# Eight buffers of e, denominators eight slots behind a chunk's end, weight bands in every sixth slot

## The chip, the cores and the metric

The kernel runs on one core of one Trainium2 chip. The time is the device time of one execution in microseconds, the median of several executions. One further execution was recorded by the hardware profiler; the views quoted below are of that one.

## What is computed

Two layers run on x of shape (2, 256, 64, 64) in fp32. Layer 0 is global attention over all 4096 pixels with eight heads of 32 channels, a fusion of the result with x by a 1x1 convolution, and a blend by a mask. Layer 1 is a channel gate, attention inside windows of 8x8 pixels, a shuffle of channels and two grouped 7x7 convolutions that make a gate.

```python
# layer 0, per image
q, k, v = proj(Wq, bq) / sqrt(32), proj(Wk, bk), proj(Wv, bv)
fuse = softmax(q @ k.T) @ v                      # 8 heads, 4096 x 4096
hybrid = conv1x1(concat([x, fuse]), Wf, bf)
x = hybrid * m + x * (1 - m)
# layer 1
x = x * sigmoid(relu(x @ ca_w1 + ca_b1) @ ca_w2 + ca_b2)
x = x + window_attention(x) @ out_w + out_b      # 8x8 windows, 4 heads
x = shuffle_channels(x)
y = relu(bn(grouped_conv7x7(x, sa_w1)))
y = bn(grouped_conv7x7(y, sa_w2))
out = x * sigmoid(y)
```

## The kernel before

A first phase projects q, k and v and stores them in DRAM. Then comes one long loop over 1024 *slots* (the for loop at L1015). A slot is one (image b, chunk c of 512 queries, group g of four heads, block m of 128 keys). With 2 images, 8 chunks, 2 groups and 32 blocks, a *chunk* is 64 slots, and there are 16 chunks. After the loop follows a tail with the last chunk's stage and the convolutions.

In slot i the loop issues the following, and the order in which instructions are issued here is the order in which each engine runs them; nothing is rearranged later.

- `scores(i + 2)`: four matmuls of k against q into PSUM (L578), and three exponentials on ScalarE into a buffer e of 128x2048 values (L588). The pool of e has `EB` = 5 buffers (L31, L585).
- `products(i)`: four matmuls of e against v that accumulate over the 32 blocks in one PSUM bank (L607), and one VectorE addition of e onto a running sum (L609), which makes the softmax denominators. The first slot of a group has no addition, since the second adds the first two e. A buffer of e is free for slot i + 5 when the matmuls and the addition of slot i are done.
- In the last slot of group 1 (slot 63 of a chunk) further work is queued with `at(delay, ...)`, which sets how many slots later it is issued: `denominators` (L630, 32 small matmuls that sum over keys, and a copy), the reciprocal on VectorE (L658), two `spread` steps (L645, matmuls that spread the reciprocals over the heads' channels, and a copy), and the product of f with the reciprocals on VectorE (L661).
- Seven slots after a chunk's end the chunk's `stage` (L664) is put in a list, and in every fourth slot the loop advances it by one of its fourteen steps (up to the next `yield`). The first step is the fusion (L674), whose matmuls read x first and then f; it ends by issuing the load of the next x on SP's queue (L518), which waits until VectorE has read the old x (L688). Later steps are the channel gate, the window attention with 16 small exponentials (L799), and last the two VectorE additions into `xo` (L861) with its stores to `x_s` (L876), nearly all on POOL's queue. The list's first step runs in slot 72 counted from the chunk's start, its last in slot 124, that is slot 60 of the next chunk.
- Loads of k and v pieces (four blocks each) go through SP's queue (L505, L507), two pieces ahead, with three buffers.
- `bands()` (L415) writes the two convolutions' weights into banded matrices `w_s` in DRAM: 156 DMAs on POOL's queue (L424, L430, L437), one in every second slot. They depend on nothing that the loop computes. The convolutions in the tail read `w_s` (L905).

POOL's queue is in order, so the band writes stand there between the stores of `xo`, which wait for VectorE.

Of the kernel before, what the change touches and what calls it, by code (L numbers as in the profile page):

```python
# [27 lines left out]
PB = 4  # L28
NPIECE = NMB // PB
AHEAD = 2  # L30
EB = 5  # L31
WB = 8
HEADS1, HD1 = 4, 64
WS = 8
# [20 lines left out]
def conv_seq_kernel(ctx: ExitStack, tc: tile.TileContext, a, out):  # L55
    nc = tc.nc
# [13 lines left out]
    def psum2(name):  # L70
        return ps["pair"].tile([P, 2, CH], F32, tag="s", name=name)
# [114 lines left out]
    with (  # L186
# [19 lines left out]
        for b in range(B):  # L206
            src = a["x"][b].rearrange("(k p) h w -> p k (h w)", p=P)
            for c in range(NCHUNK):
# [55 lines left out]
                i = b * NCHUNK + c  # L264
# [145 lines left out]
    def spread(row, n):  # L410
        f = row.shape[-1]
        return row.rearrange("p u f -> u p f").to_broadcast([NU, n, f])
# [58 lines left out]
    def pipeline(arm, shifted, pools):  # L471
# [4 lines left out]
        qp = att.enter_context(tc.tile_pool(name=f"q{arm}", bufs=2))  # L476
        ep = att.enter_context(tc.tile_pool(name=f"e{arm}", bufs=EB))

# [14 lines left out]
        stages = deque()  # L493

        def at(delay, action):
            later.append((now[0] + delay, action))

        def load_piece(n):
            if n * PB >= len(slots):
                return  # L500
            b, c, g, m = slots[n * PB]
            p = m // PB
            nm_ = f"{arm}_{b}_{c}_{g}_{p}"
            k = kvp.tile([P, PB * P], F32, tag="k", name=f"k{nm_}")
            nc.sync.dma_start(k, k_s[b, g, p])  # L505
            v = kvp.tile([P, PB, P], F32, tag="v", name=f"v{nm_}")
            nc.sync.dma_start(v, v_s[b, g, p].rearrange("p (m d) -> p m d", m=PB))  # L507
            kts[b, c, g, p], vts[b, c, g, p] = k, v

        def load_q(b, c):  # L510
            q = qp.tile([P, KC, CH], F32, tag="q", name=f"q{arm}_{b}_{c}")
            nc.sync.dma_start(q, q_s[b, c].rearrange("p (g n) -> p g n", g=KC))
            qts[b, c] = q
# [52 lines left out]
        def scores(i):  # L566
            b, c, g, m = slots[i]
            if shifted and m == 0:
                shift[0] = row_max(b, c, g)
            k, q = kts[b, c, g, m // PB], qts[b, c]  # L570
            cols = slice((m % PB) * P, (m % PB + 1) * P)
            one, pair = psum1(f"s{arm}_{i}_0"), psum2(f"s{arm}_{i}_1")
            last = psum1(f"s{arm}_{i}_2")
            heads = [one, pair[:, 0, :], pair[:, 1, :], last]
            parts = [(one, 0), (pair, slice(1, 3)), (last, 3)]
            for j in range(HG):
                r = slice(32 * j, 32 * j + 32)
                nc.tensor.matmul(heads[j], k[r, cols], q[r, g, :], start=True, stop=not shifted)  # L578
            if shifted:
                for j in range(HG):  # L580
                    r = slice(32 * j, 32 * j + 1)
                    nc.tensor.matmul(
                        heads[j], ones[r, :], shift[0][r, :], start=False, stop=True
                    )
            e = es[i] = ep.tile([P, HG, CH], F32, tag="e", name=f"e{arm}_{i}")  # L585

            def exp(tile, h):
                nc.scalar.activation(e[:, h, :], tile, AF.Exp, scale=SCALE0)  # L588

            for part in parts[:-1]:  # L590
                exp(*part)

            return lambda: exp(*parts[-1])


        def products(i):
            b, c, g, m = slots[i]
            if m == 0:
                acc[0] = avp.tile([P, CH], F32, tag="av", name=f"av{arm}_{i}")
                acc[1] = ep.tile([P, HG, CH], F32, tag="sum", name=f"sum{arm}_{i}", bufs=3)  # L600
                totals[b, c, g] = acc[1]
            av, total = acc[0], acc[1]
            e, v = es[i], vts[b, c, g, m // PB]
            start, stop = m == 0, m == NMB - 1
            for j in range(HG):
                r = slice(32 * j, 32 * j + 32)
                nc.tensor.matmul(av[r, :], v[:, m % PB, r], e[:, j, :], start=start, stop=stop)  # L607
            if m > 0:
                nc.vector.tensor_add(total, first[0] if m == 1 else total, e)  # L609
            e = es.pop(i)  # L610
            if start:
                first[0] = e
            if stop:
                if g == 0:
                    fts[b, c] = fp.tile([P, KC, CH], F32, tag="f", name=f"f{arm}_{b}_{c}")
                f = fts[b, c]
                nc.scalar.copy(f[:, g, :], av)  # L617
                if g == 0:
                    return
                both = [totals.pop((b, c, gg)) for gg in range(KC)]  # L620
                inv = fp.tile([P, P], F32, tag="inv", name=f"inv{arm}_{i}")
                rd = fp.tile([P, KC, 4, P], F32, tag="rd", name=f"rd{arm}_{i}")


                def denominators():
                    s = psum2(f"dn{arm}_{i}")
                    for h in range(HEADS0):
                        for q in range(4):
                            r = slice(32 * q, 32 * q + 32)
                            nc.tensor.matmul(  # L630
                                s[r, 0, 0:P],
                                keysum[:, h].rearrange("p i h -> p (i h)"),
                                both[h // HG][:, h % HG, q * P : (q + 1) * P],
                                start=(h == 0),
                                stop=(h == HEADS0 - 1),
                            )
                    nc.scalar.copy(inv, s[:, 0, 0:P])


                def spread(hh):  # L640
                    t = psum2(f"rd{arm}_{i}_{hh}")
                    for gg in range(KC):
                        for q in range(2):
                            r = slice(64 * hh + 32 * q, 64 * hh + 32 * q + 32)
                            nc.tensor.matmul(  # L645
                                t[:, q, gg * P : gg * P + P],
                                spread_h[r, gg].rearrange("p j d -> p (j d)"),
                                inv[r, :],
                                start=True,
                                stop=True,  # L650
                            )
                    nc.scalar.copy(
                        rd[:, :, 2 * hh : 2 * hh + 2, :],
                        t[:, :, 0 : KC * P].rearrange("p q (g n) -> p g q n", g=KC),
                    )

                at(2, denominators)
                at(3, lambda: nc.vector.reciprocal(inv, inv))  # L658
                at(4, lambda: spread(0))
                at(5, lambda: spread(1))  # L660
                at(6, lambda: nc.vector.tensor_mul(f, f, rd.rearrange("p g q n -> p g (q n)")))  # L661


        def stage(b, c):  # L664
# [329 lines left out]
        def run_later():  # L994
            for _ in range(len(later)):
                due, action = later.popleft()
                if due <= now[0]:
                    action()
                else:
                    later.append((due, action))  # L1000

        def run_stages():
            while stages:
                if next(stages[0], stages) is not stages:
                    return
                stages.popleft()
# [8 lines left out]
        for i, (b, c, g, m) in enumerate(slots):  # L1015
            now[0] = i
            if m % PB == 0:
                load_piece(i // PB + AHEAD)
            if g == KC - 1 and m == 0:
                nxt = (b, c + 1) if c + 1 < NCHUNK else (b + 1, 0)  # L1020
                if nxt[0] < B:
                    load_q(*nxt)
            rest = scores(i + 2) if i + 2 < len(slots) else None
            products(i)
            if rest:
                rest()
            if g == KC - 1 and m == NMB - 1:
                at(7, lambda b=b, c=c: stages.append(stage(b, c)))
            run_later()
            if i % 2:  # L1030
                next(banded, None)
            if i % 4 == 0:
                run_stages()
# [95 lines left out]
```

## Time and profile before

| what | value |
|---|---|
| median of 4 runs | 3165.9 us (3147.01 to 3170.44) |
| the profiled execution's own time | 3156.5 us |
| its span in the profile | 3154.7 us |
| mean granted TensorE clock | 0.984 |
| VectorE additions L609, mean of one | 2291 ns, 992 of them |
| ScalarE exponentials L588, all | 2039.9 us |
| DMA, mean over the span | 84 GB/s |

The busy time of TensorE is a model: matmuls are pipelined and their ends are computed. A wait is therefore better read from the distance between starts and from the rows that name a releaser. Where a wait has several causes, the one that came last is named. The windows of 20 us show how the band writes' stretches differ from a quiet one; the columns are the window, its length, the busy time of TensorE, weight loads, VectorE, ScalarE and POOL with instruction counts, the granted clock, the DMA share and GB/s.

```profile
880.00:900.00 20.00, 20.00 (x208) 7.20 (x205) 19.14 (x10) 17.30 (x28) 7.54 (x12) 1.00 1.03 86
900.00:920.00 20.00, 20.00 (x129) 5.83 (x131) 13.30 (x9) 13.63 (x22) 9.88 (x16) 1.00 0.92 73
920.00:940.00 20.00, 14.32 (x96) 3.68 (x94) 18.56 (x10) 11.84 (x19) 0.00 (x0) 0.83 0.62 67
...
1360.00:1380.00 20.00, 20.00 (x196) 5.91 (x192) 19.07 (x10) 16.91 (x27) 0.00 (x0) 1.00 0.18 53
```

### The profile page before, as it was taken

What the parts mean: (1) busy time and instruction counts of PE and PEld (TensorE: products, weight loads), DVE (VectorE), ACT (ScalarE), POOL (GpSimd) and SP (SyncE); (2) the same over time, 40 slices, a digit from 0 to 9 for tenths busy, and PEclk for the clock granted to TensorE, in tenths of its full rate; (3) what the DMA queues carried; (4) which work ended last, traced back from release to release, by engine and by line L of the source; (5) the groups of instructions that cost most, each with busy time, mean ns of one, the idle gap of its engine ahead of it and who ended that gap; (6) DMA issues with size and microseconds to landing.
All of it is one profiled execution on the core that took longest, in us unless ns stands there. A gap on an engine that the chain in (4) does not pass through costs nothing.

```text
span 3154.7 us, 59158 instructions
## 1 busy us (share of the span) xinstructions
PE 3030.8 (96%) x24330; PEld 1008.5 (32%) x24330; DVE 2513.5 (80%) x1341; ACT 2438.7 (77%) x4070; POOL 351.4 (11%) x595
## 2 busy tenths in 40 slices
PE   8989999999999999999999999999999999998697
PEld 4542322323222223232232322222222232322365
DVE  3339989899888888898989899898989888987111
ACT  2349888797878888888978798989898888886233
POOL 7113001102030000000000000000000000001076
PEclk9989999999999999999999999999999999999798
DMA  6956123425171313122222122221313131322274
GB/s 196 352 154 82 53 68 60 70 60 67 58 77 57 77 56 75 57 66 68 63 64 60 58 65 62 59 68 58 75 58 75 57 75 58 66 61 88 101 213 109
DMA packets 160343, 264.06 MB, mean 84 GB/s; under 512 B 43944, under 2 KB 62620, under 8 KB 160064
## 3 DMA queue, kind: packets, MB, share of 16 engines
q1 hardware_dynamic: 133664, 221.72, 24.5%
q0 software_dynamic: 22432, 35.91, 7.9%
q8 instruction: 193, 3.16, 0.4%
q10 hardware_dynamic: 3968, 2.57, 0.3%
q14 instruction: 86, 0.70, 0.1%
HBM read 197.89 MB, written 65.21 MB: 83 GB/s over the span
## 4 chain that ended last, share of the span: by engine, by line
PE 72%; DVE 6%; ACT 5%; DMA 4%; issue 3%; POOL 1%; SPq 1%; DVEq 0%; POOLq 0%
PE sa L578 30%; PE ava L607 27%; DVE suma L609 6%; PE qka L743 3%; PE hya L674 3%; ACT ea L588 2%; ACT ewa L799 2%; PE vwa L765 2%; PE opa L850 1%; DMA ka<-ks 1%; PE pta L817 1%; POOL out_dram L971 1%; SPq L971 1%; DMA wa<-ws 1%; DMA out_dram<-za 1%
## 5 line engine op out<-in xcount | busy, mean ns | idle before, releaser
L609 DVE TENSOR_TENSOR suma<-suma,ea 128x2048 f32<-128x2048 f32 x960 | 2198.9, 2291 | 106.4 <-ACT ea L588 19.5
L588 ACT ACTIVATE ea<-sa 128x512 f32<-128x512 f32 (+1 forms) x3072 | 2039.9, 744 | 93.2 <-PE sa L578 42.7
L578 PE MATMUL sa<-qa,ka 32*128 32x512 f32 x8192 | 1228.4, 643 | 47.5 <-ACT ea L588 31.9
L607 PE MATMUL ava<-ea,va 128*32 128x512 f32 x8192 | 1095.4, 607 | 0.5 <-ACT fa L617 0.5
L578 PEld LDWEIGHTS sa<-qa,ka 32*128 32x128 f32 x8192 | 347.4, 184 | 841.6 <-ACT ea L588 737.2
L607 PEld LDWEIGHTS ava<-ea,va 128*32 128x32 f32 x8192 | 161.8, 108 | 783.4 <-issue 756.8
L876 POOL DMA_DIRECT2D xs<-xo x94 | 66.0, 710 | 2462.1 <-DVE xo L861 2461.8
L963 DVE TENSOR_TENSOR za<-za,xca 128x1536 f32<-128x1536 f32 x16 | 28.1, 1759 | 149.1 <-ACT za L958 75.4
L743 PE MATMUL qka<-ua,qkv_w 128*128 128x512 f32 x256 | 119.5, 611 | 2.6 <-DVE ua L735 2.6
L971 POOL DMA_DIRECT2D out_dram<-za x192 | 108.3, 573 | 76.4 <-DVE za L963 60.8
L752 ACT ACTIVATE qka<-qka,qkv_b 128x512 f32<-128x512 f32 x64 | 40.5, 684 | 88.0 <-PE qka L743 88.0
L682 ACT ACTIVATE ta<-hya,bf 128x512 f32<-128x512 f32 x32 | 20.3, 684 | 101.4 <-PE hya L674 91.2
L686 DVE TENSOR_TENSOR ta<-ta,mca 128x512 f32<-128x512 f32 x32 | 22.0, 688 | 93.6 <-ACT ta L682 93.6
L924 PE MATMUL c1a<-xca,wa 128*32 128x384 f32 x896 | 79.2, 503 | 17.4 <-DMA xca<-xs 13.5
L794 DVE TENSOR_REDUCE mxwa<-ewa 128x16 f32<-128x1024 f32 x16 | 19.5, 1220 | 91.5 <-ACT ewa L792 91.5
L799 ACT ACTIVATE ewa<-ewa,mxwa 128x64 f32<-128x64 f32 x256 | 85.2, 346 | 1.3 <-DVE mxwa L794 1.3
L609 DVE TENSOR_TENSOR suma<-ea,ea 128x2048 f32<-128x2048 f32 x32 | 73.1, 2283 | 15.2 <-DMA xa<-in_x_dram 15.2
L946 PE MATMUL c2a<-yca,wa 32*128 32x384 f32 x896 | 79.9, 498 | 0.3 <-ACT za L955 0.3
L430 POOL DMA_DIRECT2D ws<-r2s x112 | 69.7, 624 | 90.2 <-DMA ws<-r2s 53.3
L231 ACT ACTIVATE qsq<-q,bq 128x512 f32<-128x512 f32 x32 | 22.0, 687 | 74.6 <-DVE qst L230 73.0
L955 ACT ACTIVATE za<-c2a 128x768 f32<-128x768 f32 x32 | 24.2, 808 | 66.2 <-DMA out_dram<-za 42.7
L946 PEld LDWEIGHTS c2a<-yca,wa 32*128 32x128 f32 x896 | 71.1, 303 | 10.6 <-issue 9.0
(137 smaller groups left out, 1649.6 us busy)
## 6 DMA issues: line engine op xcount, KB each, us to landing
ka<-ks SPq DMA_DIRECT2D x256, 256.0 KB
va<-vs SPq DMA_DIRECT2D x256, 256.0 KB
ws<-zero POOLq DMA_DIRECT2D x16, 896.0 KB, 23.3
wa<-ws SPq DMA_DIRECT2D x16, 896.0 KB
xca<-xs SPq DMA_DIRECT2D x32, 420.0 KB
xs<-xo POOLq DMA_DIRECT2D x78, 140.0 KB, 5.6
x<-in_x_dram SPq DMA_DIRECT2D x16, 512.0 KB
ks<-kst SPq DMA_DIRECT2D x32, 256.0 KB
```

Of the source, the lines that this page charges most:

```text
L430: nc.gpsimd.dma_start(band2[:, at0 : at0 + step * (n - 1) + 1 : step, :], spread(r2_s[k : k + 1, :, i], n),)
L578: nc.tensor.matmul(heads[j], k[r, cols], q[r, g, :], start=True, stop=not shifted)
L588: nc.scalar.activation(e[:, h, :], tile, AF.Exp, scale=SCALE0)
L607: nc.tensor.matmul(av[r, :], v[:, m % PB, r], e[:, j, :], start=start, stop=stop)
L609: nc.vector.tensor_add(total, first[0] if m == 1 else total, e)
L674: nc.tensor.matmul(s[:, oc, :], wf[:, kc, oc * P : (oc + 1) * P], xw[kc] if kc < KC else f[:, kc - KC, :], start=(kc == 0), stop=(kc == 2 ...
L743: nc.tensor.matmul(s[:, j, :], wqkv[:, kc, o : o + P], u[:, kc, :], start=(kc == 0), stop=(kc == KC - 1),)
L799: nc.scalar.activation(e[:, n, :], e[:, n, :], AF.Exp, bias=mx[:, n : n + 1], accum_out=rs[:, n : n + 1],)
L876: eng.dma_start(x_s[b, n, p + r0 : p + r1].rearrange("r g w -> g r w"), xo[64 * h : 64 * h + 64, oc, r0 - WS * c : r1 - WS * c, :],)
L924: nc.tensor.matmul(s[32 * j : 32 * j + 32, 0:n64], w[:, j, d, :], x[:, :, j, d : d + W], start=(d == 0), stop=(d == KS - 1),)
L946: nc.tensor.matmul(tiles[j // 2][:, j % 2, 0:n64], w[r, d], y[r, :, d : d + W], start=(d == 0), stop=(d == KS - 1),)
L971: eng.dma_start(dst[b, i, r0:r1, UG * u : UG * u + UG, :], z[p + r0 : p + r1, :, nb * b + n, :],)
```

## The change

Three constants of the loop's schedule are changed. The pool of e gets eight buffers of 8 KB per partition and no longer five. The denominators, the reciprocal, the two spreads and the product are issued 8, 9, 10, 11 and 12 slots after a chunk's last slot, where it was 2 to 6; with them the stage is listed 13 slots after, where it was 7, so that its first step runs in slot 76 and its last in slot 128, slot 64 of the next chunk. One of the 156 band writes is issued in every sixth slot (i = 1, 7, 13, ...), where it was every second one. The amount of work is the same. From L657 on, line numbers are one higher in the changed kernel (L658 becomes L659, and so on).

```diff
-EB = 5
+EB = 8
...
-                at(2, denominators)
-                at(3, lambda: nc.vector.reciprocal(inv, inv))
-                at(4, lambda: spread(0))
-                at(5, lambda: spread(1))
-                at(6, lambda: nc.vector.tensor_mul(f, f, rd.rearrange("p g q n -> p g (q n)")))
+
+                at(8, denominators)
+                at(9, lambda: nc.vector.reciprocal(inv, inv))
+                at(10, lambda: spread(0))
+                at(11, lambda: spread(1))
+                at(12, lambda: nc.vector.tensor_mul(f, f, rd.rearrange("p g q n -> p g (q n)")))
...
             if g == KC - 1 and m == NMB - 1:
-                at(7, lambda b=b, c=c: stages.append(stage(b, c)))
+                at(13, lambda b=b, c=c: stages.append(stage(b, c)))
             run_later()
-            if i % 2:
+            if i % 6 == 1:
                 next(banded, None)
```

## The prediction, made before the change was run

> **What bounds the kernel now.** I read the page first, then the chain of waits in order of time, then the waits and the timelines of three stretches.
>
> ```profile
> PE 3030.8 (96%) x24330; PEld 1008.5 (32%) x24330; DVE 2513.5 (80%) x1341; ACT 2438.7 (77%) x4070; POOL 351.4 (11%) x595
> ```
>
> TensorE looks full; where it still waits is the question. The chain names the fusion matmuls of every chunk (hya, L674), one period apart:
>
> ```profile
> 727.34 7.06 PE hya L674 x16
> ...
> 1075.38 7.06 PE hya L674 x16
> ...
> 1242.83 7.06 PE hya L674 x16
> ...
> 1410.28 7.06 PE hya L674 x16
> ```
>
> A clean chunk of 64 slots takes 1410.28 - 1242.83 = 167.45 us. The two chunks from 727.34 to 1075.38 take 348.04, that is 13.1 us more than two clean ones. Which wait costs that, the waits from 860 to 945 us and TensorE's timeline there say:
>
> ```profile
> PE sa L578 <- DMA ka<-ks: 5.7, 1, 5.7
> ```
> ```profile
> 931.82 2.21 PE L578 MATMUL sa<-qa,ka 32*128 32x512 f32 x8 [5.68 <-DMA ka<-ks]
> 933.96 1.93 PE L607 MATMUL ava<-ea,va 128*32 128x512 f32 x8
> ```
>
> A k piece came late, and the next matmuls ran at half speed. POOL's timeline tells what filled the DMA engines: band writes wait in POOL's order behind the xs stores, and after each store they leave in a burst, not one in two slots.
>
> ```profile
> 533.35 2.80 POOL L876 DMA_DIRECT2D xs<-xo  x4 [242.55 <-DVE xo L861]
> 536.14 1.26 POOL L430 DMA_DIRECT2D ws<-r2s  x2
> ```
>
> The waits from 225 to 390 us (chunk 0) hold the only time that ScalarE waits for VectorE, the case for more buffers of e; the same view of the clean chunk from 1410 to 1578 us has no such row:
>
> ```profile
> ACT ea L588 <- DVE suma L609: 13.5, 33, 0.7
> ```
>
> VectorE's timeline shows why: in chunk 0 it adds without a gap.
>
> ```profile
> 229.96 69.37 DVE L609 TENSOR_TENSOR suma<-suma,ea 128x2048 f32<-128x2048 f32 x29 [0.54 <-ACT ea L588]
> ```
>
> An add costs (69.37 - 2.29)/28 = 2.396 us in a row. TensorE needs 2.065 us a slot (L607 starts at 1405.08, 1407.15, 1409.22). VectorE therefore loses 0.33 us in every slot that holds no stage work and regains it where the stage puts matmuls on TensorE. So chunk 0, without a stage, is VectorE's; the later ones are TensorE's, apart from two waits at the softmax exponentials (L799), which the change doesn't touch.
>
> [...] the page has 2291 ns, and the spacing of 2.396 us is the trace's own. [...] here the DMA share is 1.03 and 0.92 in the windows from 880 to 920 us, and the next k piece, issued at 913.16, was still missing at 926.
>
> **The change part by part.** The sum is made against the profiled execution's own 3156.5 us (span 3154.7), 9.4 us under the median of 3165.9.
>
> *Bands in every sixth slot.* All 156 writes stay, and their POOL issues (0.62 us) wait for nothing on the compute engines. Before, 62 precede the first xs store and 32 follow each of the next two, 30 the third; after, 22 precede it and 10 or 11 follow each of the next stores, the last at slot 931 of 1024, long before the weights are read. In the third burst a write took (917.4 - 877.4)/30 = 1.33 us, so a burst of 8 stores and 11 writes takes about 5.6 + 14.6 = 20 us, where it took 46. What hurt was the end of the long burst meeting the load of x (L518) and the k piece queued behind it on SP; in the first 20 us of the three bursts TensorE shows 20.00 of 20 us busy. The store now leaves at slot 64 of a chunk and x some 38 us later, so the short burst is over. On SP the load of x still stands behind one k and v piece and ahead of the next, as before, since the stage moves by just four slots. Gain 13.1 us, all that the two chunks lost; at worst nothing, if each short burst still delays a piece.
>
> *Denominators, reciprocal, spreads and product six slots later.* VectorE's queue becomes: add(72), reciprocal, add(73) to add(75), product, and fusion starts right after the products of slot 76 (before: product behind add(69), fusion after slot 72). No steady chunk waits here now, so nothing is to be gained there; what counts is how late VectorE is at slots 72 and 75.
> Steady chunk: let lag be the end of add(n) less the end of products(n). Before, it is 1.5 at slot 60 and 3.5 at 63, after the xo additions (1.2) and three times 0.33. The stage now runs four slots later and its xo additions fall into slot 64, which has no add: lag at 63 is about 1.2, at 65 it is 1.2 + 1.2 + 2.4 - 4.1 = 0.7, at 71 it is 0.7 + 6 x 0.33 = 2.7. The denominators then hold TensorE 1.75 us, so lag(72) = 1.2; the reciprocal (0.95) ends 2.15 us after products(72), products(73) 2.07 after it: with 0.1 of signalling the spread waits 0.2 us. Lag(75) is then about 1.7 and the product (1.2) ends 2.9 after products(75), while fusion wants f at 2.07 + 1.4 = 3.5: 0.5 us to spare, where before it had over 6. I take 0.2 us in each of 15 chunks, 3 us, between 0 and 15 (1 us each, if my lags are short by that).
>
> *Eight buffers of e.* ScalarE may run eight slots ahead of the adds and no longer five. In steady chunks nothing changes. In chunk 0 VectorE is without a gap anyway, so TensorE only gets ahead and then meets VectorE at the reciprocal. add(65) starts at 373.68; eight adds and the reciprocal end at 373.68 + 8 x 2.396 + 0.95 = 393.8. TensorE, held by e alone (exp(71) needs add(63), done at 373.7), is through products(73) at about 383: 11 us of one wait in place of the scattered ones. Before, the first spread to fusion took 390.77 - 379.37 = 11.40 us with five slots in it; now with three, 7.3: fusion starts at 401.2 and ends at 408.3, where before the same work (fusion and slot 76) ended at 397.83 + 4 x 2.065 = 406.1. So 2.2 us are lost, and 2.2 more by the cold clock as after the wait at 926 (1.07 + 0.87 + 0.25). Together 4.4 us, between 0 and 7.
>
> *Stage four slots later at the end.* Chunk 14's last step (two additions, four stores) leaves the loop and lies under the last fusion, where VectorE waits 9.64 us. Before, TensorE waited at the last denominators:
>
> ```profile
> 2901.04 1.93 PE L630 MATMUL dna<-suma,keysum 128*32 128x128 f32 x32 [4.68 <-DVE suma L609]
> ```
>
> The xo additions (1.29) are gone from VectorE's queue there, and its last reset (the wait at L794) comes four slots later, 4 x 0.33 = 1.3: gain 2.6, between 0 and 4. The rest of the tail is a chain through DMAs that keeps its length.
>
> Sum: -13.1 + 3.0 + 4.4 - 2.6 = -8.3 us, 3148.2 for the profiled execution. For the median I let the bands' term lie between 13.1 and 22 (if the 9.4 us between profile and median are the same late pieces) and take 17: 3165.9 - 17 + 3.0 + 4.4 - 2.6 = 3153.7.
>
> **The rivals.**
> *More goes than that* (chance 0.22): the granted clock also dips to 0.91 in four windows of 20 us, three of them in the bands' time; 20 x 0.09, under 2 us each. If the bands cause those and the whole 22 us, and chunk 0 loses nothing, the time is 3165.9 - 22 - 2.6 - 5 = 3136. Against it: one dip lies at 1660 us, with no bands.
> *The bursts go on hurting* (0.14): 14 short ones cost together what the long ones did. 3165.9 + 3.0 + 4.4 - 2.6 = 3171. For it: the k piece behind x has little spare; against it: 20.00 of 20 early in each burst.
> *Slower: the spread and the fusion wait in every chunk* (0.14). One slot between add(72) and the spread, and between the product and fusion, is little if VectorE is later than I reckon; with eight buffers ScalarE no longer holds TensorE back before that. At 2.5 us a chunk: 3165.9 - 17 + 4.4 - 2.6 + 15 x 2.5 = 3188. It outweighs the gain from 1.0 us a chunk and shows as slower from 2.1. Against it: VectorE has waits of 5 us at L686 and L794 in each chunk, so no lag survives a chunk.
>
> **How the numbers follow.** The forecast, 3154 us, has the remaining 0.50; its own range is 3145 to 3166. A measurement tells about 0.5% here, so faster is under 3150 and slower over 3182. Faster: 0.22 and a quarter of the forecast's 0.50, 0.35. Slower: 0.14. Same: 0.51. The range 3132 to 3174 leaves out the slower rival and the lower end of the first.
>
> **What would show it.** Right: no wait of ScalarE for VectorE from 225 to 375 us; one wait of about 11 us of the spread for the reciprocal near 383 us; POOL bursts of 10 or 11 band writes; no TensorE wait for ka from 700 to 950 us, periods near 167.5 us throughout; the last denominators waiting about 2 us. Wrong: waits of the spread or of fusion of 1 us or more in every chunk, k pieces late in many chunks, or periods that shrink below 167, which would mean that TensorE was held by something that I haven't seen.

## The result, and the profile after

The changed kernel takes 3163.95 us (median of 34 runs, 3152.19 to 3181.0), the kernel before beside it 3161.64 us (55 runs): a ratio of 1.0009, 95% interval 0.9999 to 1.0018. That is "same", with a median 10 us above the forecast of 3154. The expected gain isn't there. The profiled execution took 3171.73 us (span 3169.9, granted clock 0.978), 15.2 us more than the one before.

First the page's line of busy times, then the chain of waits in order of time (start, length, engine, tile, line). Both are of the changed kernel.

```profile
PE 3043.7 (96%) x24330; PEld 1006.9 (32%) x24330; DVE 2515.5 (79%) x1341; ACT 2439.9 (77%) x4070; POOL 350.3 (11%) x595
```
```profile
406.27 7.06 PE hya L675 x16
578.49 7.07 PE hya L675 x16
748.92 7.07 PE hya L675 x16
...
1085.41 7.06 PE hya L675 x16
1254.44 7.06 PE hya L675 x16
1425.79 7.06 PE hya L675 x16
1594.82 7.06 PE hya L675 x16
1762.28 7.06 PE hya L675 x16
1929.73 7.06 PE hya L675 x16
...
2771.80 7.06 PE hya L675 x16
```

TensorE's busy time rose by 12.9 us with the same 24330 matmuls, so some of them ran slower. The periods say where. A clean chunk takes 167.45 us (1762.28 to 1929.73), exactly as before: the change did nothing to it. The pair of chunks that took 348.04 us before is gone. Instead six chunks take 169.03 to 169.10 (1085.41 to 1254.44), and three take 170.4 to 172.2. Over the 14 periods from the first fusion to the last the excess above 14 x 167.45 is 21.2 us, against 16.4 before.

What an extra 1.6 us is shows on TensorE's timeline. The first fence is one such chunk of the changed kernel, the second a clean chunk of it. Columns: start, length, what ran, in brackets the idle time before it and its releaser.

```profile
1337.70 1.12 PE L578 MATMUL sa<-qa,ka 32*128 32x512 f32 x2 [1.05 <-ACT ea L588]
...
1348.13 1.12 PE L578 MATMUL sa<-qa,ka 32*128 32x512 f32 x2 [1.05 <-ACT ea L588]
1349.18 1.06 PE L607 MATMUL ava<-ea,va 128*32 128x512 f32 x8
1350.18 1.96 PE L578 MATMUL sa<-qa,ka 32*128 32x512 f32 x8
1352.07 1.89 PE L607 MATMUL ava<-ea,va 128*32 128x512 f32 x8
```
```profile
1855.97 1.12 PE L578 MATMUL sa<-qa,ka 32*128 32x512 f32 x2 [1.06 <-ACT ea L588]
1857.03 1.06 PE L607 MATMUL ava<-ea,va 128*32 128x512 f32 x8
1858.02 1.14 PE L578 MATMUL sa<-qa,ka 32*128 32x512 f32 x8
1859.09 1.06 PE L607 MATMUL ava<-ea,va 128*32 128x512 f32 x8
```

Each chunk has two waits of 1.05 us where eight softmax exponentials (L800, L799 before) stand in ScalarE's queue ahead of those of the next slot. After one of these waits some chunks run about 3.4 us at half clock (1.96 for 1.14, 1.89 for 1.06) and others don't. I call this a *spell*. The matmuls behind the late k piece in the prediction, 2.21 and 1.93 us, ran so too: the granted clock was 0.50 from 929.56 to 936.39 us. Windows of 4 us with a granted clock under 0.95, grouped, give 10 spells after such waits in the changed kernel's profile and 4 in the one before. Of the 10, four follow the first wait of their chunk (489.53, 1168.67, 1509.05 and 2516.93 us) and six the second. The profile before shows the same picture, here after a first wait, in the stretch that I had put down to the bands:

```profile
812.62 1.23 PE L578 MATMUL sa<-qa,ka 32*128 32x512 f32 x2 [1.05 <-ACT ea L588]
813.79 1.93 PE L607 MATMUL ava<-ea,va 128*32 128x512 f32 x8
815.65 1.74 PE L578 MATMUL sa<-qa,ka 32*128 32x512 f32 x8
```

Now the steps that the prediction named. Chunk 0 in the waits of the changed kernel from 225 to 406 us (engine, tile and line, releaser: total, times, longest), and then on its timeline:

```profile
PE rda L645 <- DVE inva L659: 9.0, 1, 9.0
ACT ea L588 <- DVE suma L609: 5.7, 14, 0.7
```
```profile
397.02 1.01 PE L645 MATMUL rda<-inva,spread_h 32*128 32x128 f32 x6 [9.04 <-DVE inva L659]
...
399.88 1.83 PE L607 MATMUL ava<-ea,va 128*32 128x512 f32 x8
```

ScalarE's waits for VectorE fell from 13.5 us in 33 pieces to 5.7 in 14, and came back as one wait of TensorE with half-clock matmuls behind it (1.83 us for 1.06, at a granted clock of 0.50 from 397.0 to 401.5 us). VectorE adds in a row as before (29 additions in 69.38 us).

The bands on POOL's timeline: four stores and then the first of the ten writes that follow, where 32 had followed before.

```profile
548.92 2.81 POOL L877 DMA_DIRECT2D xs<-xo  x4 [311.54 <-DVE xo L862]
551.72 1.88 POOL L430 DMA_DIRECT2D ws<-r2s  x3
553.59 0.62 POOL L424 DMA_DIRECT2D ws<-r1s  x1
```

The waits of the changed kernel from 700 to 950 us hold no row of TensorE for ka. The last denominators in the tail wait 2.22 us for 4.68:

```profile
2910.65 1.08 PE L630 MATMUL dna<-suma,keysum 128*32 128x128 f32 x32 [2.22 <-DVE suma L609]
```

The 15.2 us between the two profiled executions, stretch by stretch, with equal work on both sides (four slots at 2.065 us moved where the fusion moved):

| stretch | predicted | measured | what it is |
|---|---|---|---|
| up to the first addition | 0 | +2.3 | 226.99 for 224.72 us; the projection phase, unchanged code |
| chunk 0 up to its fusion | +4.4 | +4.9 | 179.28 - 166.12 - 4 x 2.065 |
| 14 periods: spells after L799 | 0 | +11.0 | 17.5 us in ten spells for 6.5 in four |
| 14 periods: late pieces and other stalls | -13.1 | -6.2 | 3.7 us in two stalls for 9.9 with two late k pieces |
| 14 periods: spread and fusion waiting | +3.0 | 0 | no such row of TensorE |
| tail | -2.6 | +3.2 | wait -2.5; three groups of matmuls (L744, L831, L851) +4.8: 9.5, 1.6 and 5.8 us at a granted clock of 0.69, 0.50 and 0.55, for 8.0, 1.0 and 3.1 at 0.82, 1.00 and 1.00 |

The two lines of spells and stalls divide the excess of 21.2 and 16.4 us. A period with one spell alone is 1.6 us longer than a clean one. The changed kernel's first period, with two spells of which one has twice the length, is 4.8 us longer, and all of that is counted as spells. What is over in the other periods is counted as stalls. The changed kernel's two stalls are no late pieces:

```profile
740.71 1.02 PE L578 MATMUL sa<-qa,ka 32*128 32x512 f32 x2
742.22 1.13 PE L578 MATMUL sa<-qa,ka 32*128 32x512 f32 x6 [0.50 <-ACT rda L652]
...
1417.44 1.06 PE L607 MATMUL ava<-ea,va 128*32 128x512 f32 x5 [0.90 <-issue]
```

Both stand in the middle of a slot's eight matmuls, when the first ones had already read the same piece of k or v. What held TensorE there the profile doesn't say; *issue* means that it waited for nothing that is recorded.

### The profile page after: what moved, and what is told of

The parts are those of the page before. It is cut to its first block, busy times and chain, and to the rows that moved or that the text cites. A ratio compares the mean times of both kernels' runs of the same rounds, so it can differ in the third digit from the quotient of the medians.

```text
span 3169.9 us, 59129 instructions
## 1 busy us (share of the span) xinstructions
PE 3043.7 (96%) x24330; PEld 1006.9 (32%) x24330; DVE 2515.5 (79%) x1341; ACT 2439.9 (77%) x4070; POOL 350.3 (11%) x595
## 4 chain that ended last, share of the span: by engine, by line
PE 75%; ACT 5%; DVE 5%; issue 3%; DMA 2%; SPq 1%; POOL 1%; DVEq 0%; POOLq 0%
PE sa L578 32%; PE ava L607 29%; DVE suma L609 4%; PE qka L744 3%; PE hya L675 3%; ACT ea L588 2%; ACT ewa L800 2%; PE vwa L766 2%; PE opa L851 2%; DMA out_dram<-za 1%; PE pta L818 1%; SPq L972 1%; PE dna L630 1%; POOL out_dram L972 1%; DMA wa<-ws 1%
## 5 line engine op out<-in xcount | busy, mean ns | idle before, releaser
L578 PE MATMUL sa<-qa,ka 32*128 32x512 f32 x8192 | 1229.8, 645 | 40.4 <-ACT ea L588 31.8
L607 PE MATMUL ava<-ea,va 128*32 128x512 f32 x8192 | 1103.0, 610 | 1.2 <-issue 0.9
L578 PEld LDWEIGHTS sa<-qa,ka 32*128 32x128 f32 x8192 | 343.9, 184 | 840.1 <-ACT ea L588 740.7
L607 PEld LDWEIGHTS ava<-ea,va 128*32 128x32 f32 x8192 | 162.2, 108 | 789.7 <-issue 763.5
L744 PE MATMUL qka<-ua,qkv_w 128*128 128x512 f32 x256 | 121.1, 617 | 2.6 <-DVE ua L736 2.6
L609 DVE TENSOR_TENSOR suma<-ea,ea 128x2048 f32<-128x2048 f32 x32 | 73.3, 2290 | 27.2 <-DMA va<-vs 15.2
L800 ACT ACTIVATE ewa<-ewa,mxwa 128x64 f32<-128x64 f32 x256 | 85.2, 346 | 1.3 <-DVE mxwa L795 1.3
L744 PEld LDWEIGHTS qka<-ua,qkv_w 128*128 128x128 f32 x256 | 47.2, 194 | 76.8 <-issue 48.3
```

Source lines behind the costliest of these rows:

```text
L744: nc.tensor.matmul(s[:, j, :], wqkv[:, kc, o : o + P], u[:, kc, :], start=(kc == 0), stop=(kc == KC - 1),)
L800: nc.scalar.activation(e[:, n, :], e[:, n, :], AF.Exp, bias=mx[:, n : n + 1], accum_out=rs[:, n : n + 1],)
```

## The experiments

Each ran beside the kernel before on the same chip. The ratios are estimates over all runs of a pair, so they aren't exactly the quotients of the medians. Three theories stood first. A: each part has a fixed price and they add up. B: the bands cost little in a usual execution, so that the late pieces were peculiar to the profiled execution. C: with the late stage more half-clock spells follow.

**Bands in every sixth slot alone.**

```diff
-            if i % 2:
+            if i % 6 == 1:
```

> Kernel before with the band writes in every sixth slot and nothing else. Theory A (the parts add up as predicted, and the missing gain was eaten by the late denominators): the long bursts are gone and the median falls by 9 to 13 us, ratio 0.996 to 0.997, with no wait of TensorE for a k piece over 1 us. Theory B (late pieces cost little in a usual execution, and the profiled one had more of them than most): at most 3 us, ratio 0.999 to 1.000.

Measured: 3153.25 us (22 runs), ratio 0.9985 (0.9975 to 0.9994). That lies between the two expectations. The profile has five spells, and TensorE waits for no piece of k or v after chunk 0.

**Denominators and stage late, alone** (the `at` lines of the change, five buffers, bands in every second slot).

> Kernel before with only the denominators, their followers and the stage late (8 to 13 slots); five buffers of e, a band write in every second slot. Theory A: five buffers hold TensorE to three slots ahead of VectorE in chunk 0, so the wait of the spread for the reciprocal is 4 to 6 us and not 9; the band stalls stay. Together with 2.5 us won at the end the ratio is 1.000 to 1.002. Theory C (the late stage brings more spells of half clock after the exponentials L799): 5 to 10 us more, ratio 1.002 to 1.003, and more than six such spells in the profile, where the kernel before had four.

Measured: 3149.98 us, 0.9985 (0.9974 to 0.9996). The spread's wait in chunk 0 is 2.8 us; three spells. It is faster than either theory expected, and the more than six spells that C expected aren't there.

**Eight buffers alone.**

```diff
-EB = 5
+EB = 8
```

> Kernel before with only eight buffers of e. ScalarE waits for VectorE nowhere but in chunk 0, so only chunk 0 can change: TensorE runs ahead and meets VectorE at the denominators two slots behind the chunk's end, in one wait of some 7 to 10 us and at half clock behind it. Theory A: 0 to 3 us slower, ratio 1.000 to 1.001. If buffers were worth something in the steady chunks, the periods between two fusions would fall below 167.4 us; expected is that they don't.

Measured: 3159.54 us, 1.0006 (0.9995 to 1.0017). No period is shorter than 167.44 us, and chunk 0 has one wait of 8.0 us, of the denominators for the last addition.

**No band writes at all.** The 156 writes of the banded weights are left out, so the convolutions read matrices that nobody filled.

```diff
-            if i % 2:
-                next(banded, None)
```

> Kernel before without the 156 band writes: the convolutions read weights that are all zero outside the zero fill, so the output is not the reference's; the instructions of every other engine are the same. It is the upper bound of what spreading the writes can bring. Theory A: 13 to 22 us faster, ratio 0.993 to 0.996. Theory B: 4 us or less, ratio 0.9985 to 1.000.

Measured: 3155.75 us (14 runs), 0.9996 (0.9986 to 1.0006). So the writes in every second slot cost at most 0.14%, 4.4 us, with everything that follows from them. This decides for B, and against the 13.1 and 17 us of my sum. Thinner bands shouldn't gain more than no bands, so their 0.15% has to be read with its interval, which overlaps this one. Its profile has two spells and no wait for a piece after chunk 0.

**The changed kernel again, and the change with five buffers**, side by side. The second has one edit:

```diff
-EB = 8
+EB = 5
```

> The changed kernel once more, beside the other three on one chip. Theory A (each part has a fixed price and they add up: bands -0.15%, late stage between -0.15% and 0, eight buffers +0.06%) expects a ratio of 0.997 to 0.999. Theory B (bands and late stage are worth little each, and what the profiled execution of before lost to late pieces isn't lost in a usual one) expects 0.998 to 1.001. Theory C (with all three parts together more spells at half clock follow) expects 1.000 to 1.002, again nine or ten spells in the profile where before had four, and the wait of the spread for the reciprocal in chunk 0 near 9 us.

> The change with five buffers of e. If the eight buffers are what eats the gain of the other two parts (theory A), the ratio to before is 0.997 and to the changed kernel 0.995 to 0.998; the wait of the spread for the reciprocal in chunk 0 falls from 9 us to about 3. Theory B expects 0.998 to 1.000. Theory C, where the half-clock spells come by chance with the way chunks fall, expects no ordering by buffers: the time follows the mean granted clock, some 2.7 us for 0.001, and lies where that puts it.

Measured: 3164.42 us, 1.0005 (0.9988 to 1.0022), and 3161.02 us, 0.9996 (0.9983 to 1.0009). Theory A falls: by its sum the second would be at 0.997. The bands and the late stage, each 0.15% faster alone, give nothing together. The first profile has seven spells after L800, the second four. The second also has a period 9.6 us too long although its bands leave in every sixth slot:

```profile
737.86 1.02 PE L578 MATMUL sa<-qa,ka 32*128 32x512 f32 x2
745.67 2.08 PE L578 MATMUL sa<-qa,ka 32*128 32x512 f32 x6 [6.80 <-issue]
```

This isn't a late piece either, since the first two of the eight matmuls had read it. In the traces' record of DMA packets the last packet of the instruction queue (q8 on the page) before this stall and before the two of the changed kernel came 25 to 32 us after the one ahead of it, where 17 us is the median, and it landed 1.4 to 1.6 us before the stall ended. Instructions that came late would fit, but that is a guess: no run tests it. So sparse bands don't rule stalls out. Waits for a k piece are another matter: after chunk 0 TensorE has them in the loop in five of the seven profiles with bands in every second slot (0.9 to 9.5 us each) and in none of the seven with sparse bands or no bands.

**The softmax step in pairs.** If the two waits at L799 call the spells, then cutting the step finer must remove both.

```diff
-                if n % 8 == 7:
+                if n % 2 == 1:
                     yield
...
-            if i % 4 == 0:
+            if i % 3 == 0:
                 run_stages()
```

> The kernel before, but the softmax step of the window attention is cut after every second of its 16 exponentials and no longer after eight, and a stage step runs in every third slot, so that the stage still ends within a chunk. Theory: TensorE waits twice a chunk because eight small exponentials stand in ScalarE's queue ahead of those for the next slot; this costs 4.2 us a chunk in 15 chunks, 63 us, and the half-clock spells follow those waits. Then the time is 3085 to 3110 (ratio 0.977 to 0.985), the period of a clean chunk about 163.3 us, and the number of half-clock spells falls to two or fewer. Rival: ScalarE or VectorE is the true limit of the chunk (VectorE: 62 additions at 2.397 us and about 9.5 us of other work, 158 us, and its own forced waits); then the period stays above 166 and new waits for VectorE (suma, L609) appear.

> The changed kernel with the same cut of the softmax step. With the two waits gone VectorE has less time in which to catch up, so its lag grows through the chunk. If eight buffers pay where VectorE lags, this is as fast as or faster than the kernel before with the cut (by up to 0.5%). If the spread after one slot is what counts, rows of the spread waiting for the reciprocal appear in every chunk, 1 us or more each, and it is slower than that one by 0.5% or more.

Measured: on the kernel before 3156.97 us, 0.998 (0.9966 to 0.9995); on the changed kernel 3181.28 us (6 runs), 1.0056 (1.0037 to 1.0076). The waits and the spells after them are gone in the first, but the 63 us aren't there (one k piece, 7.6 us late, accounts for one period of 180.5 us in its profile). With a step in every third slot the fusions stand 63, 63 and 66 slots apart, in periods of 164.93, 164.79 and 171.02 us. Their mean is 166.91, only 0.54 under 167.45. I took the 171 for a wait, which was a misreading. In the changed kernel with this cut another wait took the place of the old ones, from 1000 to 2700 us:

```profile
PE pta L818 <- DVE ewa L810: 33.7, 10, 4.8
```

The transposes wait 4.8, 2.7 to 3.0 and 2.1 us in turn, and every chunk shows a spell. This is the "slower" mechanism of the prediction (one step later, VectorE isn't ready) at another place.

**The softmax step in fours**, with the step still in every fourth slot, on both kernels; and the pairs with an empty step ahead of the transposes.

```diff
-                if n % 8 == 7:
+                if n % 4 == 3:
```

```diff
             nc.vector.tensor_mul(e, e, rs.unsqueeze(2).to_broadcast([P, 16, 64]))
             yield
+            yield
```

> The kernel before, with the softmax step of the window attention cut after every fourth of its 16 exponentials and no longer after eight; the stage keeps its step in every fourth slot and takes 64 slots. With pairs of exponentials and a step in every third slot the two waits at L799 were gone, a clean chunk took 164.9 us for 167.45, and one half-clock spell was left of four; what it lost was one wait of the softmax transposes (L817) for VectorE in every third chunk, 6 us. Theory: the two waits cost 2.6 us a chunk (15 x 2.6 = 39 us) and call the half-clock spells; with four exponentials at a time the waits vanish too and VectorE has four slots for its part. Then the time is 3105 to 3125 (ratio 0.983 to 0.988) and its spread between executions shrinks to under 10 us. Rival: four exponentials in a row still hold TensorE up, by half as much each time but twice as often: 0.997 to 1.003.

> The changed kernel with the same cut in fours. Without the spells of half clock that fall by chance, the prices of the change itself are read here against the other kernel with this cut: if what cost the changed kernel its gain is the spells that the two waits call (theory C), it is 0 to 8 us faster than that one; if its prices are chunk 0's 5 us and the tail and nothing for the bands (theory B), it is within 5 us of it; if VectorE's lag at the spread or at the transposes counts, it is slower by 8 us or more and rows of 1 us or more for the spread or for L818 stand in every chunk.

> The kernel before with pairs of exponentials, a stage step in every third slot, and one more step of nothing between VectorE's normalising and the transposes that read it (L817), so that VectorE has six slots for it. If that wait is what made every third chunk 171 us long, all chunks take 164.8 to 165.0 us, there is no spell at half clock or one, and the time is 3115 to 3128. Rival: the wait moves to another reader; then every third chunk keeps 170 us or so, and the time stays at 3150 or more.

Measured: fours on the kernel before 3155.41 us, 0.9992 (0.9979 to 1.0006); fours on the changed kernel 3140.47 us (5 runs, 3136.7 to 3143.17), 0.9943 (0.9925 to 0.9962); pairs with an empty step 3167.65 us, 1.0028 (1.0018 to 1.0038). The last one's expectation rested on the misreading above and fell: its periods are 172.00, 166.06 and 165.91 us, apart from two with k pieces 5.1 and 9.5 us late. Why they are longer than without the empty step I didn't settle.

Of the fours, neither kernel has a wait at the softmax or a spell after it. The kernel before with fours stays at 167.42 us a clean chunk all the same (and has a k piece late by 3.9 us in the bands' part). Its waits from 1000 to 2700 us show why:

```profile
ACT ea L588 <- DVE suma L609: 24.1, 41, 1.6
```

There was no such row in the clean chunk before the change. The two waits at L799 had let VectorE catch up; without them it falls behind, all five buffers of e are full, and ScalarE waits 2.4 us a chunk. The changed kernel with fours is 15 us faster than the kernel before with fours, more than any of its expectations allowed. There this row is missing and every one of the 14 periods is 166.51 or 166.52 us. Its first fusion starts at 403.80 us and its last in the loop at 2735.00, 2331.20 us for the 14 periods where the changed kernel took 2365.5. The 34.3 us are 14 x 0.94 of the clean chunk and the 21.2 of excess, to 0.1 us.

**Fours and eight buffers, the rest as before the change**, to see which part makes 166.51 of 167.42.

```diff
-EB = 5
+EB = 8
...
-                if n % 8 == 7:
+                if n % 4 == 3:
```

> The kernel before with the softmax cut after every fourth exponential, and eight buffers of e; bands and the denominators' and stage's places as in the kernel before. With five buffers this cut left 167.42 us a chunk and 2.4 us a chunk in which ScalarE waits for VectorE's additions (L609); the changed kernel with the cut has 166.51 us in every chunk and no such wait. Theory: the eight buffers make that difference, once the two waits at L799 are gone; then steady chunks take 166.5 us here too, no wait of ScalarE for VectorE is left in them, and the time is 3138 to 3150, the upper end if late pieces in the bands' part cost as they do with five buffers. Rival: the later denominators and stage make it (VectorE's lag is spent elsewhere); then the chunks keep 167.4 us, and the time is 3152 to 3158.

Measured: 3143.56 us (9 runs), 0.9955 (0.9938 to 0.9971). All periods are 166.51 or 166.52 us but one of 169.78 in the bands' part, and no row of ScalarE for VectorE is left from 1000 to 2700 us. The eight buffers are enough; the rival falls.

The last term, how fours can save only 0.94 us a chunk when the waits were 2 x 1.05, is read from the starts of L607. First the second softmax wait of a clean chunk before the change, then the first group of four in the changed kernel with fours:

```profile
1500.80 1.06 PE L607 MATMUL ava<-ea,va 128*32 128x512 f32 x8
...
1505.03 1.07 PE L607 MATMUL ava<-ea,va 128*32 128x512 f32 x8
```
```profile
1483.02 1.06 PE L607 MATMUL ava<-ea,va 128*32 128x512 f32 x8
1484.02 1.99 PE L578 MATMUL sa<-qa,ka 32*128 32x512 f32 x8
1485.94 1.06 PE L607 MATMUL ava<-ea,va 128*32 128x512 f32 x8
```

Eight exponentials stretch a slot from 2.065 to 4.23 us, four to 2.92, where the hold no longer shows as idle but as a longer L578 (1.99 for 1.14). Per chunk 2 x 2.17 becomes 4 x 0.855, which is 0.92 us less. Most of the cost of these exponentials (eight with their sums take ScalarE 2.65 us in the changed kernel, 1334.41 to 1337.06) is work that ScalarE has to do, and only its batching can be shed.

## Why the prediction was right and where it wasn't

- *The outcome* "same" and the range 3132 to 3174 held, but that was partly luck: a gain of 12 us was forecast and none came, and both lie within the 0.5% that the prediction called "same". The sum under the forecast had one term wrong in size and one missing, and both push the same way. It also started too high: the median of four runs, 3165.9, lay 4.3 us above that of 55. With 1.3 us for the bands and nothing for the spread the same sum gives 3161.64 - 1.3 + 4.4 - 2.6 = 3162.1 us, against 3163.95 measured.
- *Bands, "Gain 13.1 us, all that the two chunks lost", and 17 for the median.* This is the step that failed. The 13.1 us hold two spells after L799 (812 and 989 us), 3.2 us; spells of this kind come without any bands too (two in the profile without band writes). The remaining 9.9 are two late k pieces and what they brought about. Those are gone, as forecast, but the changed kernel has 3.7 us in two other stalls. That the bursts held the pieces up by filling the DMA engines was my estimate, from the DMA share of 1.03 and 0.92 between 880 and 920 us; no trace shows what the k piece waited for. And for the median I took the 9.4 us between it and the profiled execution for more late pieces. 4.3 of them were the few runs of that median, and without any band write the time falls by 1.3 us (bound 4.4). Rival "bursts go on hurting" is not needed either: there was little to be gained from thinner bursts.
- *The two waits at L799, "which the change doesn't touch".* True of the waits, but I took their price as constant. It isn't: in the two profiled executions 10 spells for 4 cost 11.0 us. This term had no place in the sum.
- *Spread and fusion waiting, 0.2 us in each of 15 chunks.* Zero on TensorE. With fours, where VectorE has less time to catch up, the late places do show, in the changed kernel's waits from 1000 to 2800 us:

```profile
PEld hya L675 <- DVE fa L662: 4.2, 11, 0.4
```

  Its period is 166.51 us, though, the same as with the old places and no such row. So the slower rival's 2.5 us a chunk had no ground at this place.
- *Chunk 0, +4.4 us.* Right: 4.9, with one wait of 9.0 us (11 predicted) and half-clock matmuls behind it. "No wait of ScalarE for VectorE" was too much: 5.7 us are left.
- *Tail, -2.6 us.* Right for the wait (4.68 to 2.22 us); the tail as a whole is 3.2 us longer, mostly three groups of matmuls that fell at a lower clock in this execution (0.50 to 0.69 for 0.82 to 1.00).
- *Eight buffers of e, "in steady chunks nothing changes".* Right, though the reason is finer than given: a second limit, the waits at L799, lies within 0.03 us a chunk of the one that the buffers lift (167.45 and 167.42). Either alone changes nothing; both together give 0.94 us in every chunk and no spell.

So the expected gain was for the most part never there (the bands), chunk 0 cost more than the last denominators gave, and in the profiled execution spells came on top. What stays open is whether the change itself makes spells likelier. Their counts alone can't tell, since they depend on where the chunks fall on the clock's grid (last section). Profiles with eight buffers and the two waits show 10, 7 and 5, those with five buffers 4, 5, 3, 2 and 4. The mean granted clock of all timed executions agrees: 0.9806 and 0.9812 for the repeat and for eight buffers alone, 0.9819 and 0.9825 for the kernel before beside them. In a fit of time against clock within each of these kernels 0.001 of clock goes with some 3 us, so this would be about 4 us, an estimate. No run isolated the cause, nor why bands and late stage, each 0.15% faster alone on one chip, gave nothing together on another.

## What to carry to other kernels

Before an excess in a profile is put down to a cause, take out of it what also occurs where that cause is absent; one execution's excess is not the median's. A short, harmless-looking wait may have two further roles: it can call a spell at half clock (40 of the 224 waits of 1.05 us here did), and it can give another engine time to catch up, so that removing it uncovers the next limit at nearly the same period (167.42 us for 167.45). Where two parts each give nothing alone, try them together: cutting the softmax step in fours gave 0.9992, eight buffers 1.0006, both 0.9955, and with the whole change 0.9943.

## What the hardware showed that I had not expected

- Spells at half clock of about 3.4 us follow waits of only 1.05 us, with TensorE busy around them, and in some chunks only: in the changed kernel's profile in nine of 14 periods, with four clean ones in a row among them (1594.82 to 2264.63), the waits being the same. What decides is when a wait begins. The traces record each change of the clock, and in each of the 14 profiles all of them lie on one grid of 3.413 us. Here are three steps of it in the kernel before, with a wait from 1670.38 to 1671.43 us (columns as in the windows shown first):

```profile
1670.26:1673.67 3.41, 2.36 (x17) 0.64 (x18) 3.31 (x2) 3.41 (x9) 0.00 (x0) 1.00 0.07 28
1673.67:1677.08 3.41, 3.41 (x16) 0.40 (x13) 3.21 (x2) 2.63 (x5) 0.00 (x0) 0.50 0.00 0
1677.08:1680.49 3.41, 3.41 (x32) 0.94 (x32) 3.37 (x3) 2.44 (x5) 0.00 (x0) 1.00 0.30 77
```

  In the eight profiles with the two waits, 224 waits in all, the 40 that begin in the first half of a step (from -0.01 to 0.493 of it) are each followed by a spell, and of the 184 that begin later (0.497 to 0.981) none is. A clean chunk is 49.06 steps long, so its waits move by 0.06 of a step from chunk to chunk, and the count of spells depends, among other things, on where the loop starts on the grid: its first fusion starts at 0.15 of a step in the kernel before and at 0.39 in the changed kernel.
- The three profiles with fours, where a slot stretches to 2.92 us without an idle gap, have none after the softmax. In the eight profiles with the two waits an idle gap of 1.05 us, less than a third of a step of 3.413 us, was enough where it began in the first half of a step; it is by the grid that equal waits get unequal effects.
- Executions of one kernel spread by 13 to 30 us where there are 14 runs or more, and for most kernels the time follows the mean granted clock: for those with the two waits 0.001 of clock goes with 2.3 to 3.5 us, with a correlation of -0.82 to -0.95. Spells aren't all of it: with fours and eight buffers alone nine executions still spread by 18 us (3133.03 to 3151.41), and the profiled one shows no spell after the softmax. What makes up the rest I didn't find.
